# First image fetched as whole rows on one queue, rolled on leaving PSUM, small loads first

## The chip, the cores and the metric

The kernel runs on one core of one Trainium2 chip, in float32. The metric is the device time of one execution in microseconds (us). TensorE (PE) multiplies and transposes, VectorE (DVE), ScalarE (ACT) and GpSimd (POOL) do the rest, and SyncE (SP), ACT and POOL issue DMAs, each on a queue of its own; the core's 16 DMA engines serve all of them.

## The reference

The input x holds 16 images of 56 x 56 tokens with 384 channels. Two layers follow each other; each normalizes its input over 32 groups of 12 channels, per image, and adds its result to it.

```python
x = x + L0(_gn(x), w_qkv, w_out, b_out, rel_pos_table)   # window attention
x = x + L1(_gn(x), w)                                    # 3x3 depthwise convolution
# L0, with windows of 7 x 7 and 12 heads of 32:
x = jnp.roll(x, (-3, -3), axis=(1, 2))
q, k, v = jnp.split(x @ w_qkv.T, 3, axis=-1)
score = einsum('bhwqd,bhwkd->bhwqk', q, k) / sqrt(32) + rel   # masked at the last windows
out = einsum('bhwqk,bhwkd->bhwqd', softmax(score), v)
out = jnp.roll(out @ w_out.T + b_out, (3, 3), axis=(1, 2))
# L1: weights replaced by the sign of the clipped weights
```

The group mean and variance of an image need all of that image, so no attention on it can start before the whole image has been read.

## The kernel before

The work is cut into strips: `s` counts 16 images x 8 strips (`NS`) of 7 rows, that is 392 tokens (`ST`), and a strip has three chunks of 128 channels (`NC`). A strip in SBUF, `xs[s]`, has channels on partitions and its tokens sorted by window. A strip is worked on in two units of four windows. `all_units` walks through the 256 units in a fixed order and mixes the matmuls of neighbouring strips and the convolution of the image before into them; the order is written out by hand (`tc.manual_schedule`), so each engine executes its instructions in the order in which the program text issues them. Waits between engines are semaphores that the framework puts in from what reads and writes what.

Images 1 to 15 are loaded during the work on the image before (`fetch_halves`, `turn_halves`, `arrange`). Image 0 is different, and this is what the change is about. The block from L1046 on runs once:

- `make_room` (L135) zeroes parts of eight staging buffers: `xl0`, `xl1` and six that belong to other tensors at later times (`e`, `xn`, `vt`, `vq` and two buffers of `v`, shown as `xv`).
- `fetch` (L384) reads each of the eight strips of image 0, token by token: partitions 0 to 55 take the columns of four of its rows, partitions 56 to 111 those of the other three. The roll by three columns is made here: columns 3 to 50, 51 to 55 and 0 to 2 are three transfers, so that staging is already rolled. A strip takes six transfers (twelve where it wraps round the bottom of the image). Strip 0 goes through ACT's queue, four through SP's and three through POOL's (L1050).
- Behind the strips come `gm`, the matrix of group means, on POOL's queue, then the weights for v, q and k (`fetch_weights`), the depthwise weights and the output bias (`fetch_depthwise`), all on SP's queue, and rows of the position table (`load_bias`) on POOL's.
- `load` (L399) turns one block (strip, chunk): four PE transposes into a PSUM bank `pl`, one ACT copy that sorts the tokens by window into `xs[s]` (L412), and DVE's `bn_stats` of that copy (L416). There are four banks for this.
- `norm_products` (L331) combines the statistics: `bn_aggr` for each chunk, a group mean by PE (`pm`, 14 recorded matmuls with `gm`), then `meanwhile`, which turns the weights for v (`load_weights(2)`: PE transposes into `pw`, two DVE copies and one ACT copy to `wq_t`), then four small DVE operations on `dev` (L360 to L363), a second group mean `pv`, and a power on POOL (L366) that gives the coefficients.
- `normalize` makes `xn` on ACT, `load_weights` turns the weights for q and k, and `all_units` starts with v, q and k of strip 0. Its `meanwhile` (L1073) then turns the output weights, prepares the depthwise weights (`load_depthwise`, L185: six DVE operations on nine partitions of `accs[1]`, three PE transposes `pdw`, one DVE copy to `dw_t`), builds the bias table from the position table and the masks (`add_bias`, L229: sixteen DVE operations), and has POOL zero the convolution's buffers (`clear_conv`, L149). Only then does DVE add the bias to the first scores (L571).

Of the kernel before, what the change touches and what calls it, by code (L numbers as in the profile page):

```python
# [12 lines left out]
ALU = mybir.AluOpType  # L13
AX = mybir.AxisListType

WIN = 7
SHIFT = WIN // 2
GROUPS = 32
EPS = 1e-5
# [15 lines left out]
def kernel(  # L35
# [12 lines left out]
    nc = tc.nc  # L48
    P = 128
    B, H, W, C = x.shape  # L50
    NH = rel_table.shape[1]
    D = C // NH
    NC = C // P
    HPC = P // D
    T = WIN * WIN
    NS = H // WIN
    NW = W // WIN
    ST = WIN * W
# [34 lines left out]
    def bank(name):  # L93
        return ps.tile([P, 512], F32, tag="mm", name=name)
# [52 lines left out]
        nc.gpsimd.memset(qk[:, :, ST:], 0.0)  # L147

    def clear_conv():  # L149
        for t in (*hps, *accs, *xls):  # L150
            nc.gpsimd.memset(t, 0.0)

    def clear_again():
# [3 lines left out]
    staged = {}  # L157

    def fetch_weights(n, home):
# [5 lines left out]
            nc.sync.dma_start(wl[:, k], rows)  # L165
        staged[n] = wl

    def load_weights(n):

        for k in range(NC):  # L170
            pw = bank(f"pw_{n}_{k}")
            for c in range(NC):
                nc.tensor.transpose(pw[:, c * P : (c + 1) * P], staged[n][:, k, c * P : (c + 1) * P], ident)
            dst, r = (wq_t, NC * n + k) if n < NC else (wo_t, k)
            copy = nc.scalar.copy if k == 1 else nc.vector.tensor_copy
            copy(dst[:, :, r * P : (r + 1) * P], pw[:, : NC * P].rearrange("p (c q) -> p c q", c=NC))

    def fetch_depthwise():
        nc.sync.dma_start(
            accs[1].rearrange("p h w -> p (h w)")[:9, :C], w_dw.rearrange("a b c o -> (a b) (c o)")  # L180
        )
        for c in range(NC):
            nc.sync.dma_start(bo_sb[:, c : c + 1], b_out[c * P : (c + 1) * P].unsqueeze(1))

    def load_depthwise():  # L185
        wl = [accs[1].rearrange("p h w -> p (h w)")[:9, n * C : (n + 1) * C] for n in range(3)]
# [141 lines left out]

        nc.scalar.activation(late_tiles["dg"][:, t], ident, AF.Identity, scale=dw_t[:, NC - 1, t : t + 1])

    def norm_products(key, gm, meanwhile=None):  # L331
        st = stats.pop(key)
        name = "%d_%d" % key
        mv = small.tile([P, NC, 2], F32, tag="mv", name=f"mv{name}")
        for c in range(NC):
            nc.vector.bn_aggr(mv[:, c, :], st[:, c].rearrange("p s k -> p (s k)"))
        if key[0]:
            nc.vector.tensor_tensor(mv[:, :, 0], mv[:, :, 0], bo_sb, ALU.add)

        def group_mean(x, name):  # L340
            pg = bank(name)
            pairs = group_blocks(C, GS)
            for m in range(NC):
                of_m = [n for n, (k, j) in enumerate(pairs) if j == m]
                for n in of_m:
                    k = pairs[n][0]
                    nc.tensor.matmul(
                        pg[:, 4 * m : 4 * m + 1],
                        gm[:, n, :],
                        x[:, k : k + 1],  # L350
                        start=(n == of_m[0]),
                        stop=(n == of_m[-1]),
                    )
            return pg[:, : 4 * NC].rearrange("p (m f) -> p m f", f=4)[:, :, 0]

        mean = group_mean(mv[:, :, 0], f"pm{name}")
        if meanwhile:
            meanwhile()
        dev = small.tile([P, 3, NC], F32, tag="dev_late", name=f"dev{name}", bufs=1)
        nc.vector.tensor_copy(dev[:, 2], mean)  # L360
        nc.vector.tensor_tensor(dev[:, 0], mv[:, :, 0], dev[:, 2], ALU.subtract)
        nc.vector.tensor_tensor(dev[:, 0], dev[:, 0], dev[:, 0], ALU.mult)
        nc.vector.tensor_tensor(dev[:, 0], dev[:, 0], mv[:, :, 1], ALU.add)  # L363
        var = seen[:, B : B + NC] if key[0] else dev[:, 0]
        nc.vector.tensor_scalar(var, group_mean(dev[:, 0], f"pv{name}"), EPS, None, ALU.add)
        nc.gpsimd.tensor_tensor(dev[:, 1], var, power.to_broadcast([P, NC]), ALU.pow)  # L366
        coef = small.tile([P, NC, 2], F32, tag="coef", name=f"coef{name}", bufs=4)
        nc.vector.tensor_copy(coef[:, :, 0], dev[:, 1])
        nc.vector.scalar_tensor_tensor(coef[:, :, 1], dev[:, 2], -1.0, dev[:, 1], ALU.mult, ALU.mult)  # L369
        coefs[key] = coef  # L370
# [10 lines left out]

        return homes.get(s, xls[s % 2])

    def fetch(s, queue):  # L384
        b, r = divmod(s, NS)
        xl = staging(s)
        first = r * WIN + SHIFT
        for odd in range(2):
            t, end = 0, (WIN + 1 - odd) // 2
            while t < end:  # L390
                row = (first + odd + 2 * t) % H
                n = min(end - t, (H - row + 1) // 2)
                rows = x[b, row : row + 2 * n - 1 : 2].rearrange("t w c -> w t c")
                here = xl[odd * W : (odd + 1) * W, t : t + n, :]
                for lo, hi in ((SHIFT, SHIFT + 48), (SHIFT + 48, W), (W, R)):
                    queue.dma_start(here[lo - SHIFT : hi - SHIFT], rows[lo % W : (hi - 1) % W + 1])
                t += n

    def load(s, c):  # L399
        b, r = divmod(s, NS)  # L400
        if (0, b) not in stats:
            stats[0, b] = small.tile([P, NC, NS, 6], F32, tag="st0", name=f"st0_{b}", bufs=1)
        if c == 0:
            xs[s] = xpool.tile([P, NC, ST], F32, tag="x", name=f"x_{s}")
        pt = bank(f"pl_{s}_{c}")
        for t in range(NL):

            n = min(LT, max(ST - t * LT, HT + 1))
            nc.tensor.transpose(
                pt[:, t * LT : t * LT + n], staging(s)[:n, t, c * P : (c + 1) * P], ident[:n, :n]  # L410
            )
        nc.scalar.copy(  # L412
            xs[s][:, c, :].rearrange("p (w r c) -> p r w c", r=WIN, c=WIN),
            pt[:, :ST].rearrange("p (r w c) -> p r w c", w=NW, c=WIN),
        )
        nc.vector.bn_stats(stats[0, b][:, c, r, :], xs[s][:, c, :])  # L416

    def halves(s):
        flat = xls[s % 2].rearrange("p t c -> p (t c)")[:, : NC * NR * D]
# [626 lines left out]
    with tc.manual_schedule():  # L1046
        nc.scalar.preload_act_table_set("natural_log_exp_and_others")
        make_room()
        nc.vector.memset(score_banks, 0.0)
        for s, queue in enumerate((nc.scalar, nc.sync, nc.gpsimd, nc.sync, nc.gpsimd, nc.sync, nc.sync, nc.gpsimd)):  # L1050
            fetch(s, queue)
        gm = bpool.tile([P, BR + 2, R], F32, tag="xb", name="gm_first").rearrange("p h w -> p (h w)")
        pairs = len(group_blocks(C, GS))
        gm = gm[:, : pairs * P].rearrange("p (n q) -> p n q", q=P)
        nc.gpsimd.dma_start(gm, gmat)
        for n, home in ((2, hps[0]), (0, hps[1]), (1, accs[0])):
            fetch_weights(n, home)
        fetch_depthwise()
        clear_more()
        load_bias(nc.gpsimd, 0, 22, True)  # L1060
        for s in range(NS):
            for c in range(NC):
                load(s, c)
        fetch_weights(NC, xpool.tile([P, NC, ST], F32, tag="x", name="wl_out"))
        norm_products((0, 0), gm, lambda: load_weights(2))
        load_bias(nc.gpsimd, 22, T, True)
        normalize(0)
        for n in range(2):
            load_weights(n)
        nc.vector.memset(vt[:, :, :, T:], 0.0)  # L1070
        homes.clear()

        def meanwhile():  # L1073
            load_weights(NC)
            load_depthwise()
            add_bias(True)
            clear_conv()

        all_units(True, meanwhile)


        worst = small.tile([P, 2], F32, tag="worst", name="worst")
        for n in range(2):
            nc.vector.tensor_scalar(reach[:, n], reach[:, n], MOST[n], None, ALU.is_lt)
        nc.vector.tensor_reduce(worst[:, 0:1], reach.rearrange("p n u -> p (n u)"), AX.X, ALU.min)
        fine = small.tile([P, B + NC], F32, tag="fine", name="fine")
        nc.vector.tensor_scalar(fine, seen, 1.0e37, None, ALU.is_lt)
        nc.vector.tensor_reduce(worst[:, 1:2], fine, AX.X, ALU.min)
        pf = bank("pf")
        nc.tensor.matmul(pf[:, 0:2], ones, worst, start=True, stop=True)  # L1090
        both = small.tile([P, 1], F32, tag="both_fine", name="both_fine")
        nc.vector.tensor_reduce(both, pf[:, 0:2], AX.X, ALU.add)
        nc.vector.tensor_scalar(again, both, -1.0, 2.0 * P, ALU.mult, ALU.add)

    redo = nc.values_load(again[0:1, 0:1])
    with tc.If(redo != 0):
        with tc.manual_schedule():
# [3 lines left out]
            load_bias(nc.gpsimd, 0, T, False)  # L1101
            add_bias(False)
            for s in range(2):
                fetch(s, nc.sync)
            for s in range(NS):
                for c in range(NC):
                    load(s, c)
                if s + 2 < NS:
                    fetch(s + 2, nc.sync)
            norm_gather((0, 0), nc.sync)  # L1110
            norm_scale((0, 0), nc.sync, nc.vector)
            normalize(0)
# [45 lines left out]
```

## Time and profile before

| what | value |
|---|---|
| three runs | 4037.98, 4039.25 and 4040.57 us |
| median | 4039.25 us |
| the profiled execution, its own time | 4039.94 us |
| its span in the profile | 4038.0 us |
| PE busy | 3952.3 us (98%) |
| DVE busy | 3493.3 us (87%) |
| ACT busy | 2229.6 us (55%) |
| POOL busy | 1891.9 us (47%) |

The page gives the busy time of each engine and cuts the span into 40 slices of some 101 us; a digit is the busy share of a slice in tenths.

```profile
## 2 busy tenths in 40 slices
PE   6999999999999999999999999999999999999987
...
DVE  4556989889898998989899898998989899898897
...
PEclk8999999999999999999999999999999999999998
```

A chain of waits is followed back from the last instruction of a stretch: at each step to what released it, or to the instruction ahead of it on its engine. "issue" in it is time for which the profile shows no cause. In a timeline a line has the start, the length, the engine, the line of code, the operation with "out<-in", the number of merged instructions, and in brackets how long the engine stood idle before it and what ended that.

DVE's first 10 us are memsets of the staging buffers and of the score banks:

```profile
4.54 1.76 DVE L1049 MEMSET score_banks<- 128x2048 f32 x1 [0.43 <-issue]
```

### The profile page before, as it was taken

The numbers are of one execution on the slowest core, as the hardware profiler recorded it, in microseconds if no ns is written. First come the engines' busy times: TensorE is split into PE (matmuls) and PEld (weight loads), VectorE is DVE, ScalarE is ACT, GpSimd is POOL, SyncE is SP. The second block draws the span as 40 slices with busy tenths as digits, with TensorE's granted clock in tenths as the row PEclk, the third lists the DMA queues.
The fourth block names the chain that finished last, engine by engine and source line by source line (L and its number), as shares of the span: only waits on it lengthen the run. The fifth ranks groups of instructions, "written<-read, shape, count | busy, mean of one in ns | idle before, by whom it ended". The sixth has DMA issues, their size and how long they took to land.

```text
span 4038.0 us, 144675 instructions
## 1 busy us (share of the span) xinstructions
PE 3952.3 (98%) x63189; PEld 2414.4 (60%) x63189; DVE 3493.3 (87%) x3706; ACT 2229.6 (55%) x4654; POOL 1891.9 (47%) x3184
## 2 busy tenths in 40 slices
PE   6999999999999999999999999999999999999987
PEld 4666555555556565555556556565555656556657
DVE  4556989889898998989899898998989899898897
ACT  3545656556565655556556565655556556565552
POOL 6454545455453554545455453564545455452100
PEclk8999999999999999999999999999999999999998
DMA  4323545554554554545454554554545554553444
GB/s 104 81 68 86 115 104 123 107 124 101 113 118 106 118 119 101 117 103 123 106 127 101 115 123 100 126 111 103 116 105 121 106 125 104 114 120 80 112 101 109
DMA packets 801949, 439.35 MB, mean 109 GB/s; under 512 B 672090, under 2 KB 751483, under 8 KB 801306
## 3 DMA queue, kind: packets, MB, share of 16 engines
q1 hardware_dynamic: 711258, 267.61, 30.9%
q0 software_dynamic: 88768, 161.39, 17.2%
q8 instruction: 498, 8.16, 0.9%
q10 hardware_dynamic: 1280, 1.00, 0.1%
q14 instruction: 145, 1.19, 0.1%
HBM read 170.08 MB, written 158.45 MB: 81 GB/s over the span
## 4 chain that ended last, share of the span: by engine, by line
PE 41%; issue 18%; POOL 16%; DVE 15%; DMA 8%; ACT 2%; SPq 1%; DVEq 0%; POOLq 0%; ACTq 0%
PE pq L487 16%; POOL xl L434 11%; PE pv L500 8%; PE py L684 8%; DVE o L812 6%; PE score_banks L554 3%; PE po L645 2%; DMA xl<-in_x_dram 2%; PE score_banks L624 2%; DVE e L571 2%; DMA mvd<-mv 1%; DVE xt L451 1%; POOL dev L278 1%; DMA gt<-mvd 1%; DVE st L467 1%
## 5 line engine op out<-in xcount | busy, mean ns | idle before, releaser
L487 PE MATMUL pq<-xn,wq_t 128*128 128x392 f32 x4608 | 1584.9, 496 | 0.0
L434 POOL DMA_DIRECT2D xl<-in_x_dram x1980 | 1333.8, 728 | 134.3 <-DVE xt L451 95.4
L812 DVE SCALAR_TENSOR_TENSOR o<-hp,dw_t,o 128x1568 f32<-128x1568 f32 x752 | 1378.5, 1833 | 5.4
L487 PEld LDWEIGHTS pq<-xn,wq_t 128*128 128x128 f32 x4608 | 845.4, 188 | 595.7 <-ACT o L806 0.4
L500 PE MATMUL pv<-xn,wq_t 128*128 128x392 f32 x2304 | 815.5, 497 | 13.4 <-DVE y L692 13.4
L684 PE MATMUL py<-ot,wo_t 128*128 128x392 f32 x2304 | 818.1, 500 | 7.5 <-DVE ot L673 6.3
L494 ACT COPY qk<-pq 128x392 f32<-128x392 f32 x768 | 368.2, 483 | 562.6 <-PE pq L487 562.0
L704 POOL COPY y<-y 128x63 f32<-128x63 f32 x128 | 56.8, 444 | 1192.5 <-DVE y L692 1192.5
L684 PEld LDWEIGHTS py<-ot,wo_t 128*128 128x128 f32 x2304 | 425.0, 190 | 311.6 <-DVE ot L673 26.3
L500 PEld LDWEIGHTS pv<-xn,wq_t 128*128 128x128 f32 x2304 | 424.1, 188 | 312.9 <-DVE y L692 15.4
L589 ACT ACTIVATE e<-e 128x1176 f32<-128x1176 f32 x256 | 303.3, 1185 | 507.2 <-DVE e L571 506.1
L665 DVE SCALAR_TENSOR_TENSOR ln<-score_banks,inv 128x588 f32<-128x588 f32 x256 | 195.9, 765 | 320.7 <-ACT inv L664 318.6
L507 ACT COPY vt<-pv 128x392 f32<-128x392 f32 x384 | 189.0, 492 | 360.2 <-PE pv L500 359.4
L554 PEld LDWEIGHTS score_banks<-qk 32*49 32x49 f32 x24576 | 265.9, 118 | 145.5 <-issue 112.2
L571 DVE SCALAR_TENSOR_TENSOR e<-score_banks,bias 128x1176 f32<-128x1176 f32 x256 | 347.1, 1356 | 5.6 <-PE score_banks L554 5.6
L645 PEld LDWEIGHTS po<-e,v 49*32 49x32 f32 x24576 | 311.4, 105 | 50.8 <-issue 1.2
L463 ACT COPY x<-xt 128x196 f32<-128x196 f32 x720 | 225.6, 368 | 181.6 <-DVE xt L451 181.2
L645 PE MATMUL po<-e,v 49*32 49x49 f32 x24576 | 310.0, 212 | 0.3 <-issue 0.3
L554 PE MATMUL score_banks<-qk 32*49 32x49 f32 x24576 | 298.2, 218 | 3.3 <-DVE ln L665 2.9
L511 DVE STREAM_TRANSPOSE vq<-vt 128x512 f32<-128x512 f32 x384 | 265.8, 694 | 7.5 <-ACT vt L507 4.4
L476 ACT ACTIVATE xn<-x,coef 128x392 f32<-128x392 f32 x384 | 247.1, 711 | 6.2 <-DVE coef L369 6.2
L692 DVE TENSOR_TENSOR y<-py,x 128x392 f32<-128x392 f32 x384 | 213.4, 556 | 42.0 <-PE py L684 41.7
(176 smaller groups left out, 3318.6 us busy)
## 6 DMA issues: line engine op xcount, KB each, us to landing
v<-vq SPq DMA_DIRECT2D x2048, 48.0 KB
xb<-mid SPq DMA_DIRECT2D x90, 855.5 KB
out_dram<-o SPq DMA_DIRECT2D x736, 98.0 KB
mid<-y POOLq DMA_DIRECT2D x112, 619.5 KB
xl<-in_x_dram POOLq DMA_DIRECT2D x1260, 52.5 KB
mid<-y POOLq DMA_DIRECT2D x15, 354.0 KB
xl<-in_x_dram POOLq DMA_DIRECT2D x180, 28.0 KB
mid<-y POOLq DMA_DIRECT2D x15, 265.5 KB
```

Source lines behind the costliest of these rows:

```text
L434: nc.gpsimd.dma_start(xz[i * D + lo : i * D + hi, c, k : k + n, :], flat[token : token + n * (hi - lo)].rearrange("(k t) c -> t k c", k=n) ...
L476: nc.scalar.activation(xn[:, c, :, :T], xs[s][:, c, :].rearrange("p (w t) -> p w t", t=T), AF.Identity, bias=coef[:, c, 1:2], scale=coef[: ...
L487: nc.tensor.matmul(pq[:, :ST].rearrange("p (w t) -> p w t", t=T), wq_t[:, c, m * P : (m + 1) * P], xn[:, c, :, :T], start=(c == 0), stop=( ...
L494: nc.scalar.copy(qk[:, m, :ST], pq[:, :ST])
L500: nc.tensor.matmul(pv[:, :ST].rearrange("p (w t) -> p w t", t=T), wq_t[:, c, 2 * C + m * P : 2 * C + (m + 1) * P], xn[:, c, :, :T], start= ...
L511: nc.vector.transpose(vq[:, :, :, m].rearrange("p h n d -> p n h d"), vt[:, m].rearrange("p (n w) (j b) -> p n (w j) b", w=2, b=D),)
L554: nc.tensor.matmul(pp[row * HT : row * HT + rows, i, k0 : k0 + T], qk[part, NC * fast + j, q0 : q0 + rows], qk[part, NC * (not fast) + j, ...
L571: nc.vector.scalar_tensor_tensor(e, pp[:, :, : NC * 2 * T].rearrange("q i (n k) -> q i n k", k=T), QSCALE, bias[:, int(s % NS == NS - 1)]. ...
L589: nc.scalar.activation(flat, flat, AF.Exp, accum_out=reach[:, 0, u : u + 1])
L645: nc.tensor.matmul(po[w][i * D : (i + 1) * D, (2 * j + r) * T : (2 * j + r + 1) * T], vs[s][keys, i, n * 2 + r, j], by_head(u)[keys, i * N ...
L684: nc.tensor.matmul(py[:, :ST], wo_t[:, c, m * P : (m + 1) * P], ots[s][:, c, :], start=(c == 0), stop=(c == NC - 1),)
L812: nc.vector.scalar_tensor_tensor(acc, by_half(hp[:, dy : dy + BR, dx : dx + W]), dw_t[:, c, t : t + 1], acc, ALU.mult, ALU.add)
```

## The change

- `fetch` no longer splits a row at columns 51 and 56: one transfer takes all 56 columns of up to four rows, unrolled, and all eight strips go through SP's queue. `gm` moves from POOL's to SP's queue, between the weights for v and those for q.
- `load` makes the roll while it leaves PSUM. `bn_stats` now reads the bank itself. ACT copies the seven windows that don't wrap and then the first four columns of the last one, and DVE copies the three columns that wrap.
- `fetch_depthwise` moves to the very beginning and to ACT's queue, and `load_depthwise` moves from `meanwhile` to ahead of the strips' `load`.
- `load_weights` is split: `turn_weights` has the PE transposes. `norm_products` puts the transposes of the weights for v behind the first group mean and their copies behind the second one.
- 40 rows of the position table are issued ahead of the power on POOL, 22 before.
- `clear_conv` starts with `xls`.

```diff
+    turned = {}
+    def turn_weights(n):
+        turned[n] = [bank(f"pw_{n}_{k}") for k in range(NC)]
+        for k in range(NC):
+            for c in range(NC):
+                nc.tensor.transpose(turned[n][k][:, c * P : (c + 1) * P], staged[n][:, k, c * P : (c + 1) * P], ident)
     def load_weights(n):
+        if n not in turned:
+            turn_weights(n)
         for k in range(NC):
-            pw = bank(f"pw_{n}_{k}")
-            for c in range(NC):
-                nc.tensor.transpose(pw[:, c * P : (c + 1) * P], staged[n][:, k, c * P : (c + 1) * P], ident)
+            pw = turned[n][k]
...
     def fetch_depthwise():
-        nc.sync.dma_start(
+        nc.scalar.dma_start(
...
-            nc.sync.dma_start(bo_sb[:, c : c + 1], b_out[c * P : (c + 1) * P].unsqueeze(1))
+            nc.scalar.dma_start(bo_sb[:, c : c + 1], b_out[c * P : (c + 1) * P].unsqueeze(1))
...
         mean = group_mean(mv[:, :, 0], f"pm{name}")
-        if meanwhile:
-            meanwhile()
+        for f, n in meanwhile[:1]:
+            f(n)
...
-        nc.vector.tensor_scalar(var, group_mean(dev[:, 0], f"pv{name}"), EPS, None, ALU.add)
+        spread = group_mean(dev[:, 0], f"pv{name}")
+        for f, n in meanwhile[1:]:
+            f(n)
+        nc.vector.tensor_scalar(var, spread, EPS, None, ALU.add)
...
-                for lo, hi in ((SHIFT, SHIFT + 48), (SHIFT + 48, W), (W, R)):
-                    queue.dma_start(here[lo - SHIFT : hi - SHIFT], rows[lo % W : (hi - 1) % W + 1])
+                nc.sync.dma_start(here, rows)
...
+        nc.vector.bn_stats(stats[0, b][:, c, r, :], pt[:, :ST])
+        to = xs[s][:, c, :].rearrange("p (w r c) -> p r w c", r=WIN, c=WIN)
+        rows = pt[:, :ST].rearrange("p (r w) -> p r w", w=W)
+        cut = W - WIN
         nc.scalar.copy(
-            xs[s][:, c, :].rearrange("p (w r c) -> p r w c", r=WIN, c=WIN),
-            pt[:, :ST].rearrange("p (r w c) -> p r w c", w=NW, c=WIN),
+            to[:, :, : NW - 1], rows[:, :, SHIFT : SHIFT + cut].rearrange("p r (w c) -> p r w c", c=WIN)
         )
-        nc.vector.bn_stats(stats[0, b][:, c, r, :], xs[s][:, c, :])
+        nc.scalar.copy(to[:, :, NW - 1, : WIN - SHIFT], rows[:, :, SHIFT + cut :])
+        nc.vector.tensor_copy(to[:, :, NW - 1, WIN - SHIFT :], rows[:, :, :SHIFT])
...
-        for s, queue in enumerate((nc.scalar, nc.sync, nc.gpsimd, nc.sync, nc.gpsimd, nc.sync, nc.sync, nc.gpsimd)):
-            fetch(s, queue)
+        fetch_depthwise()
+        for s in range(NS):
+            fetch(s)
...
-        nc.gpsimd.dma_start(gm, gmat)
-        for n, home in ((2, hps[0]), (0, hps[1]), (1, accs[0])):
+        fetch_weights(2, hps[0])
+        nc.sync.dma_start(gm, gmat)
+        for n, home in ((0, hps[1]), (1, accs[0])):
             fetch_weights(n, home)
-        fetch_depthwise()
         clear_more()
-        load_bias(nc.gpsimd, 0, 22, True)
+        load_bias(nc.gpsimd, 0, 40, True)
+        load_depthwise()
...
-        norm_products((0, 0), gm, lambda: load_weights(2))
-        load_bias(nc.gpsimd, 22, T, True)
+        norm_products((0, 0), gm, ((turn_weights, 2), (load_weights, 2)))
+        load_bias(nc.gpsimd, 40, T, True)
...
         def meanwhile():
             load_weights(NC)
-            load_depthwise()
             add_bias(True)
             clear_conv()
```

## The prediction

> **What bounds the kernel now.** I read the page's 40 slices first: PE is at 9 tenths from the second slice to the third last, so between about 90 us and 3935 us the end is set by PE's own work, which the change leaves alone. What the change can give or take is how early PE reaches that state. So I read the chain of waits over the first 100 us (columns: start, length, what), then the timeline of the same stretch for what each piece waited for.
>
> ```profile
> 32.87 4.26 PE pl L409 x24
> ...
> 38.63 3.12 PE pm L347 x14
> 41.75 2.04 PE pw L173 x9
> 43.79 0.02 issue
> 43.81 0.56 DVE wq_t L176
> ...
> 45.17 3.12 PE pv L347 x14
> 48.29 3.55 PE pw L173 x18
> ...
> 70.73 0.56 DVE wo_t L176
> 71.28 1.15 DVE o L187
> ...
> 75.32 0.07 DVE dw_t L196
> ...
> 75.72 3.03 DVE bias L238 x9
> ```
>
> The chain waits for the last strip of x until 32.87, turns two strips (24 transposes), then runs two group means (pm, pv) with weight transposes between them, then q, k, v, and at 70.7 a row of DVE work: six operations on the depthwise weights, then the bias table. Each of these three places is touched. The timeline shows how one block (strip, channel chunk) passes three engines:
>
> ```profile
> 15.55 4.58 PE L409 MATMUL pl<-ident,xl 112*128 112x112 f32 x24 [15.55 <-DMA xl<-in_x_dram]
> 16.48 0.52 ACT L412 COPY x<-pl 128x392 f32<-128x392 f32 x1 [14.46 <-PE pl L409]
> 17.03 1.91 DVE L416 BATCH_NORM_STATS2 st<-x 128x6 f32<-128x392 f32 x3 [10.72 <-ACT x L412]
> ...
> 87.18 0.69 ACT L655 COPY ot<-po 128x294 f32<-128x294 f32 x2
> ```
>
> PE writes PSUM, ACT copies it out, DVE takes statistics of the copy while ACT is at the next block. A handoff costs 0.03 us (17.00 to 17.03). The last line gives what ACT saves when nothing stands between two copies: each takes 0.398 alone, both 0.69, so neighbours overlap by 0.10. DVE's 16 bias additions (0.444 each, 5.86 together) show the same, 0.083.
>
> **Part 1: the fetch.** 24 issues leave POOL and 6 leave ACT; 18 transfers of 56 columns stand on SP, with gm and all weights behind them. Before, x came from about 2.6 to 32.7 us: 4.82 MB (8 strips of 7 rows of 56 columns, 3136 packets of 1536 B) in 30.1 us, 160 GB/s, while the DMA engines were busy 0.97 of that stretch. Two rules of the Trainium skill speak against the new shape. "DMA: Bandwidth & Descriptors", section "Why a DMA increments its semaphore by 16 and not by 1", says that a transfer runs on the largest number up to 16 that divides its outer size: 56 columns use 14 engines, 48 use 16. The trace agrees on the old pieces: ACT's queue shows 440 packets, 392 of data and 48 = 16+5+3+16+5+3 small ones. "SBUF — State Buffer", section "Door 1: The DMA port swizzle", says partitions 0 to 63 reach half of the ports. By the rows, the weights, over all 128 partitions, came at 359 GB/s (34 to 36 us) and x at 160. By the port rule the fullest port gets 8 of 56 partitions, an estimate of 190 GB/s and 25 us; by the row, with 14 of 16 engines, 140 GB/s and 34 us. So x is complete between 28 and 37 us; I take 30, because one queue mixes no short pieces of 3 and 5 columns. It turns out to matter little:
>
> **Part 2: leaving PSUM.** In the changed program as built, the waits of a block form a ring. DVE's bn_stats (now of PSUM) waits for PE. ACT's first copy (343 elements) waits for DVE's count after that bn_stats, not for PE. ACT's second copy (28 elements) follows. DVE's copy of 21 elements waits for ACT's count, and stands on DVE ahead of the next block's bn_stats. So the two engines take turns, and nothing overlaps from block to block:
> - bn_stats 0.57 (the L416 row: 0.569; DVE's 384-element copy from PSUM takes 0.557, so PSUM adds nothing) + handoff 0.03
> - first copy: the 392-element row takes 0.514; less 49 elements at 0.00087 (L494 0.483 at 392 against L655 0.398 at 294) 0.47, less overlap 0.10: 0.37
> - second copy: not in the trace; between 0.17 (the same slope at 28) and 0.213 (L466, 21 elements from SBUF): 0.19; handoff 0.03
> - DVE copy: 0.185 (L196, 27 elements from PSUM) less overlap 0.085: 0.10
>
> That is 1.29 us a block, 31.0 for 24. Bounds: 1.20 (all at their low ends) and 1.47 (no overlaps).
>
> **Part 3: depthwise weights first.** They now stand ahead of all that: on DVE after the memset that ends at 6.30 (4.54 + 1.76), and PE's pdw transposes stand ahead of the first strip. ACT's four issues land long before; ACT computes nothing until then. The six operations: L188 to L192 ran from 72.46 to 74.82, plus 0.38 for the first (its 1.15 now lies beside a POOL memset of the same tile, 70.60 to 72.21; if it recurs, 0.8 later): 9.05. pdw to dw_t took 0.46: PE is free at 9.5. First transposes to first reader took 0.93 (15.55 to 16.48): first bn_stats at 10.4. The cover is gone here: without this step the ring could start when strip 0 is in, near 7.
>
> Ring: 10.4 + 31.0 = 41.4, and pm follows 0.45 after the first aggregate (38.18 to 38.63 before): 41.85. **Before: 38.63, so 3.2 later**, though x may be complete well before that. The last strip's first block starts at 10.4 + 21 x 1.29 = 37.5, so PE needs it at 36.6; x at 30 hides behind the ring. gm and the weights (1.05 MB) follow x by some 3 us at 359 GB/s, also before 41.85.
>
> **Part 4: pm to pv.** Before 45.17 - 38.63 = 6.54, as the chain ran through DVE's copies of wq_t, queued ahead of dev. Now dev comes first, hidden (0.7) by PE's 2.04 of pw: 3.12 + 2.04 + 0.02 = 5.18. **Gain 1.36.** The copies move behind pv's 3.12. POOL's power has 40 row issues ahead of it (40 x 0.51 = 20 us from about 2), done by 25, and 9 instead of 27 behind it.
>
> **Part 5: after q and k.** DVE goes from wo_t straight to the bias: 75.72 - 71.28 = **4.44 gained**. What is late next is the bias itself (5.9) and exp; PE's scores need only 1.5. rel and mask are issued earlier (9 x 0.5 after the power, before 27 x 0.5). POOL's memsets no longer wait for pdw (3.1 us), and POOL starts image 1's fetch about 10 us earlier; PE did not wait for it, 0.
>
> **Clock.** Granted clock was 0.50 from 31.05 to 51.5. From 41.85 on PE now has no pause (before: 1.4 before pv). If pm and pw count as busy, full clock comes within the 10 us before v, worth up to 2 (pv and pw at the transposes' 392 against 222 to 260 ns); if weight-load-bound pm does not count, 0 or a few tenths lost. I take 0.8 gain.
>
> **Sum** against the profiled execution of 4039.94 (span 4038.0): +3.2 - 1.36 - 4.44 - 0.8 = -3.4: 4036.5. The runs' median is 0.7 below that execution: **4036**.
>
> **Rivals.**
> 1. *The copies overlap after all* (or a wait is weaker than I read): a block then costs the busier engine about 0.6, and the blocks keep up with x. pm stood 5.9 after the last strip (32.73); less 2.1 (one strip to turn, not two) and 0.5 (no copy ahead of the statistics) that is 3.3: with x at 28 to 30, 31.3 to 33.3, so 5.3 to 7.3 earlier and 6.6 more from parts 4, 5 and the clock: 4039.94 - 11.9 to 13.9 - 0.7, say 4026.5. For it: ACT and DVE do overlap now. Against: the waits named above.
> 2. *The single queue is the bound, and it is slower*: beyond 36.6 each us of x costs one. The trace has a stretch of 1.5 us at 100 GB/s (22.5 to 24 us); if 14 engines at half the ports gave that throughout, x is in at 2.6 + 48.2 = 50.8, 14.2 past the point: 4050. It ends slower than before from 40 us on, and by over 0.2% from 48.
> 3. *The gain at the bias is repaid*, because PE restarts at half clock (it did from 82.25 to 89.08) one window later: 4.8 us of such work can shift by 3.4: 4038 to 4039.
>
> **Numbers.** Forecast 0.70, rival 1 0.09, rival 2 0.08, rival 3 0.13. The forecast's own range: ring -2.2 to +4.3, clock -1.2 to +0.8, start -0.4 to +0.9; together 4031 to 4041.5. For 8 in 10 I go to 4030 and 4042.5. A difference under 0.2% (8.1 us) cannot be told from none here: faster needs 4031.1. Rival 1 and the forecast's low end give 0.14 faster; rival 2's far half and unseen waits 0.08 slower; 0.78 the same.
>
> **What would show it.** Right: bn_stats, two ACT copies and a short DVE copy in turn, 1.25 to 1.35 us a block, DVE idle before the short copy "<-ACT"; pm at 41 to 43; pv 5.2 after pm; the bias directly after wo_t; x in by 36. Wrong: a block near 0.7, PE waiting for DMA at the last strips, or pm before 36 or after 46.

## The result, and the profile after

Twelve runs of the changed kernel have a median of 4038.38 us (4036.02 to 4040.2), twelve of the kernel before, on the same chip, 4040.31 (4037.98 to 4043.75). The ratio is 0.9994, with a 95% interval of 0.9985 to 1.0003: no difference that can be told from none, as forecast (4036.0, within 4030 to 4042.5). The profiled execution's span went from 4038.0 to 4037.2.

On the page the 40 slices hardly moved; of PE's, DVE's and the clock's, as they were shown of before:

```profile
## 2 busy tenths in 40 slices
PE   7999999999999999999999999999999999999987
...
DVE  4656989899898998989899898998989899898897
...
PEclk9999999999999999999999999999999999999998
```

Only the first slice differs in PE's row and in the clock's (7 for 6, 9 for 8), and there everything happened. The clock's 9 is no gain: the changed kernel's trace has no record of the clock before 52.2 us, and the page counts that time as full, though PE ran at half speed in it (see the clock below). In the timeline of the changed kernel, the first blocks, in the manner of the lines shown of before (start, length, engine, line, operation, and in brackets the idle time before it and what ended it):

```profile
10.44 0.57 DVE L423 BATCH_NORM_STATS2 st<-pl 128x6 f32<-128x392 f32 x1 [0.67 <-PE pl L420]
...
11.05 0.47 ACT L427 COPY x<-pl 128x343 f32<-128x343 f32 x1 [9.03 <-DVE st L423]
...
11.62 0.18 DVE L431 COPY x<-pl 128x21 f32<-128x21 f32 x1 [0.61 <-ACT x L430]
11.72 0.56 DVE L423 BATCH_NORM_STATS2 st<-pl 128x6 f32<-128x392 f32 x1
```

ACT had been idle for 9.03 us and yet began only when DVE's statistics were done (10.44 + 0.57 = 11.01); DVE then stood for 0.61 until ACT had done both copies. From 10.44 to 11.72 one block takes 1.28; the 24 blocks keep to 1.26 to 1.28 up to the last at 39.62. Further on:

```profile
41.50 3.12 PE L356 MATMUL pm<-mv,gm_first 128*128 128x1 f32 x14 [4.55 <-DVE mv L345]
44.26 1.97 PEld L175 LDWEIGHTS pw<-ident,hp 128*128 128x128 f32 x9
44.48 2.16 PE L175 MATMUL pw<-ident,hp 128*128 128x128 f32 x9
...
46.43 2.98 PE L356 MATMUL pv<-dev,gm_first 128*128 128x1 f32 x14
...
72.33 5.85 DVE L247 TENSOR_TENSOR bias<-rel,mask 128x147 f32<-128x147 f32 x16
...
80.82 1.24 PE L639 MATMUL score_banks<-e,ones 49*32 49x294 f32 x16 [5.77 <-ACT e L604]
```

The last line is the moment when PE restarts after waiting for the first exponentials. In the kernel before it was

```profile
84.32 1.24 PE L624 MATMUL score_banks<-e,ones 49*32 49x294 f32 x16 [4.48 <-ACT e L589]
```

The steps in turn (pm and pv are the two group means, pq the products for q and k, 36 a strip):

| step | before | after | difference so far |
|---|---|---|---|
| first mean, pm | 38.63 | 41.50 | +2.87 |
| second mean, pv | 45.17 | 46.43 | +1.26 |
| q begins (pq) | 57.70 | 58.82 | +1.12 |
| bias begins | 75.72 | 72.33 | -3.39 |
| PE restarts with the first sums (L639, before L624) | 84.32 | 80.82 | -3.50 |
| q of strip 1 begins (37th pq) | 92.98 | 89.97 | -3.01 |
| last of the 256 exponentials begins | 3931.86 | 3929.56 | -2.3 |
| end of the span | 4038.0 | 4037.2 | -0.8 |

The start is 3.5 us better, and in these two executions the rest of the program gives most of it back, the last 1.5 us behind the last exponential. The table by windows (columns: window, its length, then busy us and count for PE, weight loads, DVE, ACT and POOL, then the granted TensorE clock, DMA share and GB/s) shows there, for after and then for before, the stretch at half clock before the last full one:

```profile
3991.20:3998.00 6.80, 5.86 (x27) 5.86 (x28) 6.69 (x5) 4.33 (x5) 0.00 (x0) 0.50 0.58 108
```

```profile
3993.70:3997.10 3.40, 3.40 (x17) 3.40 (x18) 3.36 (x3) 3.22 (x4) 0.00 (x0) 0.50 0.41 62
```

After had 5.86 us of PE's work at half speed there, before 3.40; at full clock the difference would be half as long, an estimate of 1.2 us. That the change causes this is not shown: over the fourteen profiled executions of this study the time from the last exponential to the end goes from 106.1 us (before) to 109.9, after has 107.6, and executions with the short stretch at half clock range from 106.1 to 109.5.

### The profile page after: what moved, and what is told of

It reads as the page before. It is cut to its first block, busy times and chain, and to the rows that moved or that the text cites. A ratio compares the mean times of both kernels' runs of the same rounds, so it can differ in the third digit from the quotient of the medians.

```text
span 4037.2 us, 144682 instructions
## 1 busy us (share of the span) xinstructions
PE 3956.5 (98%) x63189; PEld 2416.3 (60%) x63189; DVE 3494.4 (87%) x3730; ACT 2228.2 (55%) x4678; POOL 1863.1 (46%) x3159
## 3 DMA queue, kind: packets, MB, share of 16 engines
q0 software_dynamic: 87648, 159.12, 16.6%
## 4 chain that ended last, share of the span: by engine, by line
PE 38%; issue 19%; POOL 17%; DVE 14%; DMA 7%; ACT 2%; SPq 1%; DVEq 0%; POOLq 0%; ACTq 0%
PE pq L502 15%; POOL xl L449 12%; PE py L699 8%; PE pv L515 8%; DVE o L827 6%; PE score_banks L569 3%; PE po L660 2%; DMA mvd<-mv 2%; DMA xl<-in_x_dram 2%; PE score_banks L639 2%; DVE e L586 2%; DVE xt L466 1%; POOL dev L287 1%; DMA gt<-mvd 1%; DMA cod<-both 1%
## 5 line engine op out<-in xcount | busy, mean ns | idle before, releaser
L515 PE MATMUL pv<-xn,wq_t 128*128 128x392 f32 x2304 | 815.0, 497 | 13.6 <-DVE y L707 13.6
```

The costliest lines, as they stand in the source:

```text
L515: nc.tensor.matmul(pv[:, :ST].rearrange("p (w t) -> p w t", t=T), wq_t[:, c, 2 * C + m * P : 2 * C + (m + 1) * P], xn[:, c, :, :T], start= ...
```

## The experiments

Each version was timed beside the kernel before, and the ratio is taken to that. "us" beside a ratio is the ratio's distance from 1 times 4041, so that versions timed beside different runs of the kernel before can be compared; by that measure after stands at -2.4.

**e1: the order on DVE.** after, with the statistics behind the copies in `load`:

```diff
-        nc.vector.bn_stats(stats[0, b][:, c, r, :], pt[:, :ST])
...
         nc.vector.tensor_copy(to[:, :, NW - 1, WIN - SHIFT :], rows[:, :, :SHIFT])
+        nc.vector.bn_stats(stats[0, b][:, c, r, :], pt[:, :ST])
```

> The changed kernel with one line moved: bn_stats stands behind the three copies of its block, not ahead of them. Theory (the ring of waits sets the pace): ACT then waits for PE alone and runs ahead of DVE, a block costs 0.6 to 0.7 us instead of 1.27, the blocks keep up with x (complete near 28.7 us), pm starts near 32.7 instead of 41.5, and the median is about 8.8 us below the changed kernel, near 4029.6. Rival (the fetch or PE bounds this stretch): pm stays near 41, no difference.

Measured: 4030.98, ratio 0.9975 (0.9964 to 0.9985), -10.1 us. Its timeline:

```profile
11.02 0.18 DVE L430 COPY x<-pl 128x21 f32<-128x21 f32 x1 [1.25 <-ACT x L429]
11.12 0.47 ACT L426 COPY x<-pl 128x343 f32<-128x343 f32 x1
11.12 0.56 DVE L431 BATCH_NORM_STATS2 st<-pl 128x6 f32<-128x392 f32 x1
11.48 0.18 ACT L429 COPY x<-pl 128x28 f32<-128x28 f32 x1
```

ACT's next copy now starts in the same moment as the statistics of the block before, 11.12. The same instructions take 0.67 us a block within a strip instead of 1.27; between strips DVE waits for x. pm comes at 33.88 instead of 41.50, and PE restarts at 74.11 instead of 80.82. The ring of waits is shown: one line's place was worth 6.7 us at the restart and 7.7 by the ratios, and with it the change is a gain of 0.25%.

**e2 and e6: the old fetch and load.** What is left of the change are the small loads and the depthwise weights at the beginning and the weights turned ahead of pv. e6 differs from e2 only in the table rows that POOL issues ahead of its power:

```diff
-                nc.sync.dma_start(here, rows)
+                for lo, hi in ((SHIFT, SHIFT + 48), (SHIFT + 48, W), (W, R)):
+                    queue.dma_start(here[lo - SHIFT : hi - SHIFT], rows[lo % W : (hi - 1) % W + 1])
...
# e6 alone
-        load_bias(nc.gpsimd, 0, 40, True)
+        load_bias(nc.gpsimd, 0, 22, True)
```

> The changed kernel with fetch and load of before (columns 48, 5 and 3 on three queues, one ACT copy, statistics of the copy): what is left of the change are the small loads first, the depthwise weights first, the split weight turn and the rows of the position table. Theory: x in near 32.7 us, pm near 38.6 as before, pm to pv 4.9 instead of 6.5, bias right after wo_t: about 6 us below before, near 4034.3, so below the changed kernel by 4. Rival (the small loads first delay the three queues, or the gain at the bias is given back as half clock): within 2 us of before.

> e2_old_load with 22 table rows ahead of POOL's power, as before had it, instead of 40. Theory (in e2_old_load the gain of the parts left in, depthwise first and bias after wo_t, was lost because POOL came to the power only at 50.7, behind 40 row issues): pv's mean to v's product takes 3.4 us again instead of 6.7, the time is about 3.3 us below e2_old_load and 5 below before, a ratio near 0.9989. Rival (the gain went elsewhere): it stays at e2_old_load's 0.9997.

Measured: e2 4040.3, ratio 0.9997 (0.9989 to 1.0006), a miss; e6 4036.82, ratio 0.9992 (0.9984 to 1.0001). The reason stands in POOL's rows of e2's timeline:

```profile
42.24 8.45 POOL L227 DMA_DIRECT2D rel<-_conv_rel_pos_table_dram  x17 [0.23 <-issue]
...
50.70 0.91 POOL L378 TENSOR_TENSOR dev<-dev,power 128x3 f32<-128x3 f32 x1
```

and in e6's:

```profile
44.76 0.89 POOL L378 TENSOR_TENSOR dev<-dev,power 128x3 f32<-128x3 f32 x1 [4.95 <-DVE dev L377]
```

In e2 the mean pv was there at 47.04, but POOL was issuing table rows until 50.70; in e6 it had been idle for 4.95 us and took the power 0.25 after DVE. From the mean's end to v's first product took 6.7 us in e2, 3.4 in e6, as the theory said. The times don't decide it: by the ratios e6 is 2.0 us below e2, less than the intervals are wide. In the trace e6 is 5.9 us ahead at v: 3.3 here, 1.8 as its pm met the full clock, 0.7 with x. In after the 40 rows do no harm, because POOL has no strips to issue. e6 against after, -3.2 and -2.4 us, can't be told apart: no gain of the new fetch and load, as they were built, over the old ones shows.

**e3: the depthwise weights back behind q and k.**

```diff
-        load_depthwise()
         for s in range(NS):
...
         def meanwhile():
             load_weights(NC)
+            load_depthwise()
             add_bias(True)
```

> The changed kernel with the preparation of the depthwise weights back at its old place, after q and k; their load stays first. Theory: the ring starts when strip 0 is in, near 7 instead of 10.4, pm near 38; the six operations are paid between wo_t and the bias (4.4): about 1 us above the changed kernel, near 4039.4. Rival (x is late for the ring, so its start doesn't matter): pm stays at 41.5, 4.4 us above, near 4042.8.

Measured: 4040.23, ratio 0.9995 (0.9987 to 1.0004). The time can't tell this from after; the trace can. The ring starts at 8.06 instead of 10.44 (pm 39.16 instead of 41.50), and the bias begins 5.27 after the last pq instead of 1.50. So the early place costs 2.3 us at pm, of which 1.3 are left where q ends (69.55 against 70.83), and gains 3.8 behind it: PE restarts at 80.82 with it and at 83.32 without, 2.5 us in its favour.

**e4 and e7: the rows of 56 columns on three queues.** e4 has the queues of before, e7 gives strips 0 and 1 to SP and strip 5 to ACT.

```diff
-        for s in range(NS):
-            fetch(s)
+        for s, queue in enumerate((nc.scalar, nc.sync, nc.gpsimd, nc.sync, nc.gpsimd, nc.sync, nc.sync, nc.gpsimd)):
+            fetch(s, queue)
```

> The changed kernel with its whole rows of 56 columns spread over the three queues as before. Theory: the fetch hides behind the ring, so pm stays at 41 to 42 and the median at that of the changed kernel within 1 us, whether x comes faster or slower, as long as it is in by 36.6. Rival (the fetch on one queue sets the stretch): pm moves with the arrival of x.

> e4_three_queues with strips 0 and 1 on SP's queue and strip 5 on ACT's. Theory (the whole loss of e4_three_queues is strip 0 arriving at 19.9 behind ACT's small loads; the ring of waits then runs at its own 1.27): first statistics at about 10.4, pm at about 41.5, the time as after within 1 to 2 us. Rival (the strips on three queues come too late or out of order for the ring anyway): pm later than 43 and the time 2 us or more above after.

Measured: e4 4053.12, ratio 1.0029 (1.0018 to 1.004); e7 4046.19, ratio 1.0013 (1.0006 to 1.002). In both the theory missed and the rival held. PE's row in e4, then in e7:

```profile
21.28 4.65 PE L420 MATMUL pl<-ident,xl 112*128 112x112 f32 x24 [11.55 <-DMA xl<-in_x_dram]
```

```profile
25.57 2.24 PE L420 MATMUL pl<-ident,xn 112*128 112x112 f32 x12 [6.53 <-DMA xn<-in_x_dram]
```

In e4 strip 0 stands on ACT's queue behind three loads of 128 four-byte packets each, which pass until 8 us, and then shares the DMA engines with two other queues: it is in at 21.28, the ring starts 11.8 us late and ends as late. In e7 strip 0 is in time, but strip 3, third on SP, comes at 25.57 and holds the ring for 3.5 us; strip 1 had held it for 1.1. So three queues ran the strips against each other, and the ring, which needs them in order and takes its 1.27 a block in any case, can't make up a wait. The old load could: in e2 strip 0 came as late (21.17), and pm stood at 39.09. To the ring one queue in order is worth 4.7 us (e7) to 11.8 (e4) at pm, although its x is in later (29.6 us against 28.5 and 27.9).

**e5: halves side by side.** e1, with the odd rows of each strip (partitions 56 to 111) on POOL's queue and half of the table rows ahead of the power:

```diff
-                nc.sync.dma_start(here, rows)
+                (nc.gpsimd if odd and homes else nc.sync).dma_start(here, rows)
```

> e1_order with the odd-row halves of the strips (partitions 56 to 111) on POOL's queue and the even-row halves on SP's, and 20 instead of 40 table rows ahead of POOL's power. Theory (one DMA of 56 partitions at a time is what holds the fetch at 190 to 200 GB/s; two halves at once go side by side): x is in at 17 to 20 us instead of 28.7, the blocks follow at 0.60 to 0.67 us each, pm at 25 to 27.5, and the time is about 7 us below e1_order, a ratio near 0.9957. Rival (14 engines, the queue or the memory set the rate, however the halves are issued): x still comes in at about 28, pm stays near 33, no gain over e1_order.

Measured: 4029.97, ratio 0.9976 (0.9968 to 0.9983), no gain over e1. The answer lies between the two expectations: 236 GB/s where both halves ran (10 to 20 us), against 196 for one (e1, 2 to 28 us). pm came at 31.20, and PE restarted 3.87 us before e1's. At the 37th pq 2.28 of it was left: PE was at half clock to 76.9, 6.7 us after the restart, in e1 only 3.4.

**e8, e9 and e10: the half clock after the restart.** after, e5 and e1, each with 36 transposes that nothing reads, where PE waits for the first exponentials:

```diff
+    def keep_warm(n):
+        pw = bank("warm")
+        for i in range(n):
+            nc.tensor.transpose(pw[:, :P], ident, ident)
...
+                    if fast and u == 0:
+                        keep_warm(36)
                     if fast:
                         add_up(u)
```

> after with 36 transposes of the identity into an unused bank on TensorE between pv of strip 1 and the first sums, where TensorE was idle for 5.77 us (75.05 to 80.82). They are worth 4.6 us at 0.127 each, end near 79.7 and delay nothing. Theory (the half clock after the restart, 80.82 to 86.3, takes back part of what the earlier start gained): TensorE is at the full clock from the restart, the 5.5 us of half-speed work become 2.7, and the time is 2.7 us below after, a ratio to before near 0.9987. Rival (that work is bound by other engines, or the clock falls later instead): the 37th pq starts where it did, 9.2 us after the restart, and the time is after's.

> e5_halves with the same 36 transposes. There the half clock lasted from before the restart at 70.24 to 76.9. Theory: 6.7 us of half-speed work become 3.3, the restart to the 37th pq takes 6.3 us instead of 9.7, and the time is about 3.3 below e5_halves, a ratio near 0.9968. Rival: as e5_halves.

> e1_order with the same 36 transposes. There the half clock lasted 3.4 us after the restart at 74.11. Theory: 1.7 us below e1_order, a ratio near 0.9971, and 3.9 us above e9_warm_halves, which is what the earlier restart of the halves is worth once the clock is the same (3.87 at the restart; of it only 2.3 was left at the 37th pq in e5_halves against e1_order). Rival: as e1_order, and no further from e9_warm_halves than e1_order was from e5_halves.

In e8's timeline:

```profile
74.95 4.09 PE L1003 MATMUL warm<-ident 128*128 128x128 f32 x36
80.88 0.73 PE L639 MATMUL score_banks<-e,ones 49*32 49x294 f32 x16 [1.84 <-ACT e L604]
```

In e8 the sums take 0.73 instead of 1.24, and the 37th pq follows 7.19 us after the restart instead of 9.15. So the half clock took 1.96 us from after's early gain. Yet the times barely move: e8 4037.62, ratio 0.9991 (0.9982 to 1.0); e9 4029.83, 0.9971 (0.9959 to 0.9982); e10 4029.39, 0.9968 (0.9956 to 0.9981). Each is 0.3 to 0.7 thousandths below its kernel without the transposes, inside the intervals. By the exponentials, e8 leads after by 1.9 us at the fifth and by 1.1 at the last. Whether the rest is lost for a reason or by the scatter of single executions is open. The 3.9 us that e9 should have over e10 did not come either: it restarted at 71.95 and e10 at 73.27, since its strips came later than e5's had (pm 31.66, and at half clock, 3.12 us instead of 1.92) and e10's sooner than e1's (32.85).

**e11 and e12: two rows in one DMA.** Rows 2t and 2t+1 lie one behind the other in x, so a pair of rows is 112 tokens for 112 partitions. e11 is e10 with this fetch, e12 is after with it.

```diff
+        flat = x[b].rearrange("h w c -> (h w) c")
...
+            rows = flat[row * W : (row + 2 * n) * W].rearrange("(t q) c -> q t c", t=n)
+            nc.sync.dma_start(xl[: 2 * W, t : t + n, :], rows)
```

> e10_warm_order with each strip's full pairs of rows fetched by one DMA to 112 partitions (two neighbouring rows lie one behind the other in x), still on SP's queue alone and in order. Theory (what holds the fetch at 190 to 215 GB/s is that each DMA writes 56 neighbouring partitions): the rate goes to that of the weights, which go to 128 partitions in rows of the same 1536 bytes at 343 to 384 GB/s, x is in at 16 to 18 us, the blocks follow at 0.67 without waits, pm at 26 to 27.5 instead of 32.9, the ratio near 0.9955. Rival (the 112 destinations are not it: e5_halves reached only 227 to 247 with both halves under way): 200 to 250 GB/s, x in at 22 to 28, pm at 29 to 33, the ratio 0.996 to 0.9968.

> after with the same fetch by pairs and nothing else changed. Theory (the ring of waits sets after's pace, the end of the fetch does not): the pitch stays at 1.27, pm at 41.5, the time is that of after, a ratio near 0.9994, even if x is in 10 us earlier. Rival (the fetch has a part in it): pm earlier than 40.5.

Measured: e11 4023.88, ratio 0.9959 (0.9945 to 0.9972), -16.6 us, the lowest of the study, though its interval overlaps e10's; e12 4039.43, ratio 0.9998 (0.9989 to 1.0007). The DMA view of after from 2 to 28 us, and of e11 from 2 to 20:

```profile
DMA packets 4709, 5.09 MB, mean 196 GB/s; under 512 B 1441, under 2 KB 4703, under 8 KB 4709
```

```profile
DMA packets 3989, 4.37 MB, mean 243 GB/s; under 512 B 1170, under 2 KB 3989, under 8 KB 3989
```

The rate rose by a quarter, as the rival had it, not to the 353 GB/s of the weights (e11, 24 to 30 us); x was in at 23.7. For the blocks of e11 that was nearly enough:

```profile
16.14 0.56 DVE L433 BATCH_NORM_STATS2 st<-pl 128x6 f32<-128x392 f32 x1
...
16.70 0.56 DVE L433 BATCH_NORM_STATS2 st<-pl 128x6 f32<-128x392 f32 x1
```

They follow each other every 0.56 to 0.67 us, from 13.8 to 24.1 us with PE at full clock, and wait only at the last strips; pm comes at 27.27, so that pm and the ratio fall where the theory had them. e12 had x in at 24.9, 4.7 us before after, and kept its 1.27 a block and pm at 41.55: in the ring an earlier x is worth nothing.

## Why the prediction was right

- **Part 1, the fetch.** The last of x landed at 29.6 us; the text said 28 to 37 and took 30. In e1, which has the same fetch, PE waits for it:

```profile
30.21 1.87 PE L420 MATMUL pl<-ident,xv 112*128 112x112 f32 x10 [0.44 <-DMA xv<-in_x_dram]
```

From its first packet at 2.3 that is 176 GB/s for x, nearer to the port rule's estimate (190 GB/s) than to the row's (140). But e11 speaks against the rule as the whole cause: by the Trainium skill, "SBUF — State Buffer", section "Door 1: The DMA port swizzle", partitions 0 to 111 reach every one of the 16 ports, and the rate was still 243 GB/s against 353 for the weights in the six us behind (24 to 30 us), on the same queue, in rows of the same 1536 bytes. One row in seven still went to 56 partitions; six parts at 353 and one at 176 would make 308, by estimate. What holds x back besides is open. "It turns out to matter little" holds for the end of the fetch (e12); it overlooked that the order on one queue is what gives the ring its strips in time (e4, e7).
- **Part 2, the ring.** Forecast 1.29 us a block, measured 1.26 to 1.28. e1 shows that the waits named there are the cause: with the order changed, 0.67. ACT waits for DVE's statistics though both only read. The Trainium skill, "PSUM — Partial Sum Buffer", section "PSUM bank collisions raise a hardware error", says that two engines must not be in the same PSUM bank and quadrant at once, reads included, and that the compiler's scheduler puts a dependency between them. The order in the traces agrees: in after ACT starts 0.04 us behind the statistics of the same bank, in e1 it copies the next bank while DVE is in the one before. That this rule is what put the waits into this program is not shown. The lower bound of 1.20 a block does not come out of the terms listed: with each at its low end they give 1.27, which is what was measured.
- **Part 3, depthwise first.** Statistics from 10.4 forecast, 10.44 measured; pm 41.85 and 41.50. The cover that the text named as gone, "the ring could start when strip 0 is in, near 7", shows in e3: 8.06.
- **Part 4, pm to pv.** 5.18 forecast, 4.93 measured, 6.54 before. "POOL's power has 40 row issues ahead of it, done by 25" was too early, since POOL waited for earlier rows to land between the issues: the last of the 40 ended at 36.08. It did no harm (POOL was idle for 13.6 us before the power), and e2 showed how thin that was: with POOL's strips in front, the rows were done only at 50.7.
- **Part 5, the bias.** From the first q to the bias before 18.02, after 13.51: 4.51 gained where 4.44 was forecast. e3 confirms the place.
- **The clock: wrong.** The term assumed that PE without a pause from 41.85 on would reach full clock early enough ahead of v, for 0.8 us. PE had no pause, but nine transposes `pw` took 2.16 both at 44.48 and at 49.27, against 1.14 at full clock (70.67), and the granted clock is on record as full only from 52.2; before had it from 51.3. From pv to v's first product took 6.39 us, 6.52 before: 0.1 of the 0.8 was there. In after's timeline:

```profile
49.27 2.16 PE L175 MATMUL pw<-ident,hp 128*128 128x128 f32 x9
51.23 1.63 PE L175 MATMUL pw<-ident,o 128*128 128x128 f32 x9
...
70.67 1.14 PE L175 MATMUL pw<-ident,wl_out 128*128 128x128 f32 x9
```

The change of speed falls into the second of these groups. In all fourteen traces the full clock comes between 0.7 us before and 2.2 us after v's first product, however early pm began (27.3 to 53.3 us). Transposes alone do bring it up, as e11 shows:

```profile
9.48 4.27 PE L422 MATMUL pl<-ident,xl 112*128 112x112 f32 x24
...
16.95 1.55 PE L422 MATMUL pl<-ident,vt 112*128 112x112 f32 x12
```

PE did nothing else there but three small transposes at 9.09, the granted clock is on record as full from 13.8, and twelve transposes went from half of 4.27 to 1.55. So what did not bring it up ahead of v is probably the one-column work of pm and pv; no run leaves them out. By the Trainium skill, "TensorE: Matmul & The Clock Gate", section "Part 1: The HAM clock gate (the "warmup" mystery)", one busy window of some 3.4 us, which does not start with the work, brings the full clock: by 48.3 at the latest, an estimate of two windows from 41.5 on. The trace shows it some 4 us later, so this work did not count as busy in the page's sense, or the page's window is not all of it. The side of the text that said "if weight-load-bound pm does not count" was the right one.
- **Rival 3** was partly true at the same time: 0.5 of the 3.5 us at the restart were gone at the 37th pq, and e8 shows that 1.96 us lay in that half clock in all. The tail took another 1.5 in the profiled execution. The text's 3.4 us is half the length of the stretch that it names; the trace has that stretch from 82.0 to 88.8, 0.24 us earlier than the text, and one more at half clock, from 75.2 to 78.6, that the text leaves out.

The sum: forecast -3.4, measured -3.5 at PE's restart, -3.0 at the 37th pq, -0.8 at the end of one execution, -1.9 between the medians, with -6.1 to +1.2 as the interval of the ratio in us. Parts 2 to 5 were right one by one. That the restart agrees to 0.1 us is luck in part: most of the 0.8 of the clock was missing, and pm, pv and the bias came some tenths better each. The ends of the text's own range, -3.8 and +6.0 by its terms, make 4032.2 to 4042.0 and not 4031 to 4041.5; the result lies within either. Neither the clock nor the tail can be settled further by runs that scatter by 4 us: the times show that the change is worth less than 0.2%, not that it is worth 3 us.

## What to carry to other kernels

When two engines read one PSUM tile, look in the timeline at whether they overlap from block to block: if each waits for the other's last read, the order in which one engine's reads are issued sets the pace, and moving one line (e1) was worth more than the whole change. A change that "does nothing" can hold two large effects of opposite sign: take the parts apart by milestones in the trace before dropping it. For a first load that feeds a chain which can't make up a wait, put it on one queue in the order of use (e4, e7), in DMAs over as many partitions as the layout allows (e11, where pm came 5.6 us earlier than in e10).

## What the runs showed of the hardware, unexpected

- Rows of 1536 bytes from x came at 196 GB/s to 56 partitions (after, 2 to 28 us) and at 243 to 112 (e11, 2 to 20 us), those of the weights at 353 to 128 (e11, 24 to 30 us). A packet of x took some 113 ns in after and 102 in e11, one of the weights 69.
- One-column matmuls behind weight loads (pm) took 3.12 us for 14 in after, but 1.92 in e5, where the granted clock was full from 25.7 to 32.5: they run at the clock that they find, and a PE busy with them and with `pw` for 7.9 us (41.5 to 49.4) did not bring it up. e5's timeline, where pm still met the full clock and pw, pv did not:

```profile
31.20 1.92 PE L356 MATMUL pm<-mv,gm_first 128*128 128x1 f32 x14 [2.07 <-DVE mv L345]
32.99 2.16 PE L175 MATMUL pw<-ident,hp 128*128 128x128 f32 x9
34.94 2.98 PE L356 MATMUL pv<-dev,gm_first 128*128 128x1 f32 x14
```

- 36 transposes in a pause of 5.8 us kept the clock full over it (e8); the pause of 1.84 us that was left did not lower it. In after the same pause left it at half from 79.5 to 86.3.
